# Two-layer Newton and spectral-convolution kernel: pacing the normalisation statistics of layer 0, and a round between dependent operations on different engines

## The chip, the cores and the metric

One Trainium2 chip, one of its cores. The metric is device time in microseconds of one execution, median over runs. TensorE is called PE, VectorE DVE, ScalarE ACT, GpSimd POOL and SyncE SP; PSUM is the matmul accumulator, eight banks.

## The reference

The input `x` has 32 batches of 32 channels of 128x128 float32 images. Each layer normalises and adds its result to its input:

```python
def _gn(v, G=16, eps=1e-5):
    ...
    return ((g - m) / jnp.sqrt(s + eps)).reshape(v.shape)

# layer 0: Newton iterations towards a matrix square root of each 128x128 image
normA = jnp.sqrt(jnp.sum(A2 * A2, axis=(1, 2)))
Y = A2 / normA[:, None, None]
...
for _ in range(NUM_ITER):
    T = 0.5 * (3.0 * I - jnp.matmul(Z, Y))
    Y = jnp.matmul(Y, T)
    Z = jnp.matmul(T, Z)
...
x = x + _L0_conv_ref(_gn(x))
# layer 1: FFT, 32x32 low modes mixed over channels, inverse FFT
x = x + _L1_conv_ref(_gn(x), L1_conv_weights1, L1_conv_weights2)
```

For this case only the shape of the work matters: layer 0 needs, before it can start on a batch, statistics of that batch's input (a sum of squares per channel and mean and variance per pair of channels, with two square roots on the way). Layer 1 needs the same kind of statistics of layer 0's output, with one square root, and then transforms, small channel products and an inverse transform.

## The kernel before, in words

**Sets.** A set is four channels of one batch: 8 sets a batch, 256 in all. `newton` (L398 on) takes a set through layer 0: ten groups of matmuls for a far set and twelve for a near one (below), almost all into one PSUM bank each, each read out by DVE (L280, L425) or ACT (L272, L404, L407, L418, L421) into the operand of the next. It yields between the groups.

**Rounds and lanes.** The main loop at the end of the function writes the program in rounds. In a round each of up to nine lanes advances its set by one step, and between the lanes other queues advance by a step: `norms` (a set's normalisation, `staged`), `preps` (statistics of layer 0, after lane 1), `specs` (statistics and spectrum of layer 1, after lane 2), `posts`, `prods` and `backs` (channel products and inverse transforms of layer 1). A `yield` in one of these generators ends its step, so what follows is written down a round later. A scheduler orders the instructions of each engine by the order of writing and by when it believes operands to be there; instructions in `kept(...)` keep their order. So each engine's queue is fixed before the run.

**Two stages.** The sets of batches 1 to 18 are "far": one transposition goes through DRAM and POOL (L373 to L386), nine lanes are in use and a set starts every 3 rounds (`FAR`). Those of batch 0 and of batches 19 to 31 are "near": that transposition is on PE, about five lanes are in use and a set starts every 5 rounds (`NEAR`). While `early` is open, up to the 158th finished set (`MORE`), extra buffers exist; then `change()` closes it and opens the buffers of layer 1's products and inverse transforms. That is the second stage here: from about 1,680 us on, layer 0's near sets run side by side with `wide_products`, `small_products` and `inverse` of layer 1. The batches of layer 1 go in groups of 20, 7, 3 and 2 (`GROUPS`); a group's products begin when the spectrum of its last batch is done.

**Statistics of layer 0.** `prep` (L185) does two batches at a time. It loads 16 pieces of 256 KB on ACT's DMA queue (L198, tile `xs`, four buffers, three loads ahead), takes two `bn_stats` of each (L206, one step a piece), then `moments` (two small matmuls, L170 and L214, and a few DVE operations), `root` (L154: a square root on ACT, four DVE operations), a reciprocal, `root` again, and the factors. Counted in the code, the results are there after 24 steps. `stage` (in the main part) adds a `prep` to the queue when the set named in `coming` is staged: for batches b, b+1 that is set 4 of batch b-2. They are needed when set 0 of batch b is staged, 12 sets later.

**Layer 1's part.** `settle` folds a finished set and takes its `bn_stats` (L443). `summed` (L484 on) and `spectrum` (L516 on) run in `specs` once a batch. In `summed` the DVE reciprocal L506 follows the ACT square root L505; in `spectrum` the small DVE operation L551 follows the ACT read-out L545 of the same tile. `inverse` reads four banks: the ACT copies L895 (tile `d`) take one half of each bank and the DVE additions L900 (tile `yt`) the other.

Of the kernel before, what the change touches and what calls it, by code (L numbers as in the profile page):

```python
# [37 lines left out]
B = 32  # L38
# [13 lines left out]
FIRST = GROUPS[0] - 1  # L52
# [16 lines left out]
def conv_preact_kernel(  # L69
# [56 lines left out]
    early = first.enter_context(tc.tile_pool(name="early", bufs=1, side="right"))  # L126
# [21 lines left out]
    def bank():  # L148
        return ps8.tile([P, 4, P], F32, tag="ps", name="ps")

    def root(v, n, tag):

        s0 = small.tile([P, n], F32, tag="root_0", name=f"{tag}_s0")
        nc.scalar.activation(s0, v, AF.Sqrt)  # L154
        q = small.tile([P, n], F32, tag="root_1", name=f"{tag}_q")
        nc.vector.reciprocal(q, s0)
        nc.vector.tensor_mul(q, q, v)
        nc.vector.tensor_tensor(q, q, s0, ALU.add)
        s = small.tile([P, n], F32, tag=f"{tag}_s", name=f"{tag}_s", bufs=2)
        nc.vector.tensor_scalar_mul(s, q, 0.5)  # L160
        return s
# [23 lines left out]
    def prep(bs, made):  # L185

        n = len(bs)
        nc_, ng = n * C, n * G
        first_b = bs[0]
        st = small.tile([P, ng, 6], F32, tag="a_st", name=f"a_st{first_b}", bufs=2)  # L190
        tiles = []
        parts = [(b, i) for b in bs for i in range(C // 4)]

        def load(k):
            b, i = parts[k]
            t = stp.tile([P, 2, 2 * P], F32, tag="xs", name=f"xs{b}_{i}")
            src = xs_in[b, :, 2 * i : 2 * i + 2].rearrange("p g h c -> p g (h c)")
            kept(nc.scalar.dma_start(out=t, in_=src))  # L198
            tiles.append(t)

        for k in range(3):
            load(k)
        yield
        for k in range(len(parts)):
            for j in range(2):
                nc.vector.bn_stats(st[:, 2 * k + j, :], tiles[k][:, j, :])  # L206
            yield
            if k + 3 < len(parts):
                load(k + 3)
        ms = small.tile([P, ng], F32, tag="a_ms", name=f"a_ms{first_b}")  # L210
        nm, d = yield from moments(st, ms, "a")
        yield from pause
        pq = bank()[:, 0, 0:nc_]
        nc.tensor.matmul(pq, avg_mean, d.rearrange("p g c -> p (g c)"), start=True, stop=True)  # L214

        v = small.tile([P, nc_ + ng], F32, tag="a_v", name=f"a_v{first_b}")
        nc.vector.tensor_scalar_mul(v[:, 0:nc_], pq, -512 / (P * P))
        yield
        vg = small.tile([P, ng], F32, tag="a_vg", name=f"a_vg{first_b}")
        nc.vector.tensor_reduce(  # L220
            vg, v[:, 0:nc_].rearrange("p (g c) -> p g c", c=2), AX.X, ALU.add
        )
        nc.vector.tensor_scalar(v[:, nc_:], vg, 0.5, EPS, ALU.mult, ALU.add)
        s = root(v, nc_ + ng, "a_r")
        iv = small.tile([P, nc_ + ng], F32, tag="a_inv", name=f"a_inv{first_b}")
        nc.vector.reciprocal(iv, s)
        yield

        sc = small.tile([P, nc_], F32, tag="a_sc", name=f"a_sc{first_b}", bufs=2)
        nc.vector.tensor_scalar_mul(sc, iv[:, 0:nc_], MS / P)  # L230
        nn = small.tile([P, ng, 2], F32, tag="a_d", name=f"a_n{first_b}")
        nc.vector.tensor_tensor(  # L232
            nn,
            s[:, 0:nc_].rearrange("p (g c) -> p g c", c=2),
            iv[:, nc_:, None].to_broadcast([P, ng, 2]),
            ALU.mult,
        )
        nn = nn.rearrange("p g c -> p (g c)")
        nc.vector.tensor_scalar_mul(nn, nn, P * (1.5 / (EYE * QF)) ** 2)
        sn = root(nn, nc_, "a_t")  # L240

        off = small.tile([P, ng, 2], F32, tag="a_off", name=f"a_off{first_b}", bufs=2)
        nc.vector.tensor_tensor(
            off,
            sc.rearrange("p (g c) -> p g c", c=2),
            nm[:, :, None].to_broadcast([P, ng, 2]),
            ALU.mult,
        )
        off = off.rearrange("p g c -> p (g c)")
        for k, b in enumerate(bs):  # L250
            g, c = slice(k * G, k * G + G), slice(k * C, k * C + C)
            made[b] = (nm[:, g], sc[:, c], off[:, c], sn[:, c])
        yield
# [60 lines left out]
    def is_far(b):  # L314
        return 0 < b < FIRST
# [168 lines left out]
    def summed(b, st):  # L484

        mq = small.tile([P, 2, G], F32, tag="b_mq", name=f"b_mq{b}")
        _, d = yield from moments(st, mq[:, 0, :], "b")
        yield

        nc.vector.tensor_reduce(mq[:, 1, :], d, AX.X, ALU.add)  # L490
        wide = small.tile([P, 2, G, 2], F32, tag="b_wide", name=f"b_wide{b}")
        nc.vector.tensor_copy(wide, mq[:, :, :, None].to_broadcast([P, 2, G, 2]))
        wide = wide.rearrange("p k g c -> p k (g c)")
        yield from pause
        pv = bank()[:, 0, :]
        for i in range(4):
            rows = slice(C * i, C * i + C)
            nc.tensor.matmul(pv[rows, 0:1], wide[:, 1, :], avg_v, start=True, stop=True)
        nc.tensor.matmul(pv[0:C, 1:2], wide[:, 0, :], avg_0, start=True, stop=True)
        v = small.tile([P, 2], F32, tag="b_v", name=f"b_v{b}")  # L500
        nc.vector.tensor_scalar(v[:, 0:1], pv[:, 0:1], 1.0, EPS, ALU.mult, ALU.add)
        nc.vector.tensor_copy(v[0:C, 1:2], pv[0:C, 1:2])
        yield
        s = small.tile([P, 3], F32, tag="b_r", name=f"b_r{b}")
        nc.scalar.activation(s[:, 0:1], v[:, 0:1], AF.Sqrt)  # L505
        nc.vector.reciprocal(s[:, 1:2], s[:, 0:1])  # L506
        nc.vector.tensor_scalar(
            s[:, 2:3], v[:, 0:1], s[:, 1:2], s[:, 1:2], ALU.mult, ALU.mult
        )
        nc.vector.tensor_scalar(s[:, 2:3], s[:, 2:3], -0.5, 1.5, ALU.mult, ALU.add)  # L510
        r = small.tile([P, 1], F32, tag="b_inv", name=f"b_inv{b}")
        nc.vector.tensor_mul(r, s[:, 1:2], s[:, 2:3])
        scales[b] = v, r
        yield

    def spectrum(b, u):  # L516
# [16 lines left out]
        for i in range(2):  # L533
# [7 lines left out]
        v, r = scales.pop(b)  # L541
# [6 lines left out]
            AF.Identity,  # L548
            scale=r,
        )  # L550
        nc.vector.scalar_tensor_tensor(  # L551
            spec[0:C, 0, 0, 0:1], v[0:C, 1:2], r[0:C], spec[0:C, 0, 0, 0:1], ALU.mult, ALU.add
        )
        yield
        i, j = where[b]
# [375 lines left out]
    rounds = 0  # L931
# [59 lines left out]
    def finish(queue):  # L991
        while queue:
            yield

    preps.append(prep([0], made))
    coming = [((0, 0), [1])] + [((b - 2, 4), [b, b + 1]) for b in range(2, B, 2)]
    fetch(*fetches.pop(0))
    stage()
    fetch(*fetches.pop(0))
    while todo or any(lanes) or posts or specs or prods or backs:  # L1000
        tail = not todo and not any(lanes)
        if early and len(settled) >= MORE:
            change()
        for i in range(LANES):
            step(norms)
            step(loads)
            far = todo and is_far(todo[0][0])
            under_way = [is_far(lane[0]) for lane in lanes if lane]
            room = far or under_way.count(False) + 0.6 * under_way.count(True) < LESS
            if lanes[i] is None and todo and room and rounds >= due:  # L1010
                due = max(due, rounds - 1) + (FAR if far else NEAR)
                while norms:
                    step(norms)
                b, g = todo.pop(0)
                xt = ready[0][0]
                lanes[i] = (b, g, xt, newton(g, made[b][3], *ready.pop(0), far, has_more(b, g)))
                if stages:
                    stage()
                if not todo:
                    loads.append(weights())  # L1020
            if lanes[i] is not None:
                b, g, xt, steps = lanes[i]
                if (b, g) == (B - 1, C // 4 - 1):
                    steps_of_last.append(rounds)
                if next(steps, lanes) is lanes:
                    lanes[i] = None
                    end(b, g, xt)
            if i == 1:
                step(preps)
            if i == 2 or tail:  # L1030
                step(specs)
            if i == 3 or tail:
                step(posts)
            if i == 0 and rounds % 3 or tail:
                step(prods)
            if i == 0 and (rounds % 3 == 0 or holding) or tail and not (posts or specs):
                step(backs)
        rounds += 1
# [69 lines left out]
```

## Time and profile before

| quantity | value |
|---|---|
| time, median of 3 runs | 3051.56 us (3039.80 to 3056.13) |
| the profiled execution's own time | 3040.36 us |
| its span, first to last instruction | 3038.6 us |
| PE busy | 2893.8 us (95%) |
| DVE busy | 2219.3 us (73%) |
| POOL busy | 1997.6 us (66%) |
| ACT busy | 1636.0 us (54%) |
| mean granted PE clock | 0.984 |
| DMA, mean rate | 209 GB/s |

The busy time of PE counts the time in which at least one matmul is under way, with modelled ends, so that the count of matmul instructions started in a stretch says more than the busy share. One float32 product of 128x128 by 128x128 is two such instructions. Times within the span are counted from its start.

### The profile page before, as it was taken

How to read it: one execution, taken by the hardware profiler on the slowest of the kernel's cores; microseconds unless marked ns; L12 is line 12 of the kernel's file. 1: busy time of each engine (PE TensorE's matmuls, PEld its weight loads, DVE VectorE, ACT ScalarE, POOL GpSimd, SP SyncE). 2: the span in 40 equal slices, each digit the busy share in tenths (PEclk: the TensorE clock that was granted, in tenths of full speed). 3: DMA queues.
4: the chain of work that ended last, by engine and by line, in shares of the span. 5: the costliest groups of instructions: out<-in, count | busy, mean ns of one | idle time of the engine just before them, and what ended most of it. 6: DMA issues, size and time to landing. Idle time of an engine off the chain costs nothing.

```text
span 3038.6 us, 73447 instructions
## 1 busy us (share of the span) xinstructions
PE 2893.8 (95%) x27076; PEld 2684.5 (88%) x27076; DVE 2219.3 (73%) x4255; ACT 1636.0 (54%) x4187; POOL 1997.6 (66%) x2312
## 2 busy tenths in 40 slices
PE   6999999999999999999999999899999998999994
PEld 6899999999999999999999889798898887899983
DVE  6778787978787878778776745876877765876664
ACT  3565656565655656566544445455454454555552
POOL 4567677667777676777766435667677774677453
PEclk9999999999999999999999999999999999999996
DMA  5476766667675767576742566667667767775676
GB/s 179 148 224 199 220 213 205 212 207 224 197 237 188 251 184 246 185 229 198 228 136 81 183 204 214 232 206 239 229 225 242 245 231 242 227 222 189 198 240 217
DMA packets 476659, 636.40 MB, mean 209 GB/s; under 512 B 97040, under 2 KB 257296, under 8 KB 476304
## 3 DMA queue, kind: packets, MB, share of 16 engines
q1 hardware_dynamic: 363408, 425.88, 43.3%
q10 hardware_dynamic: 112896, 205.83, 21.4%
q8 instruction: 217, 3.56, 0.5%
q14 instruction: 138, 1.13, 0.1%
HBM read 402.42 MB, written 229.11 MB: 208 GB/s over the span
## 4 chain that ended last, share of the span: by engine, by line
PE 75%; DMA 10%; DVE 9%; POOL 2%; issue 2%; ACT 2%; SPq 1%; ACTq 0%; DVEq 0%; POOLq 0%
PE ps L305 49%; PE ps L415 12%; PE ps L311 6%; DMA w<-turn 3%; DMA xs<-in_xs 3%; PE ps L461 2%; PE ps L883 2%; DMA or<-od 1%; PE ps L612 1%; DVE yt L900 1%; PE ps L865 1%; DVE a_st L206 1%; DVE v L280 1%; DVE turn L371 1%; PE ps L682 1%
## 5 line engine op out<-in xcount | busy, mean ns | idle before, releaser
L386 POOL TENSOR_TENSOR w<-w,r 128x512 f32<-128x512 f32 x288 | 366.2, 1275 | 316.2 <-DMA w<-turn 262.1
L305 PE MATMUL ps<-w,v 128*128 128x128 f32 x4096 | 554.4, 279 | 19.0 <-POOL w L386 12.1
L339 ACT ACTIVATE b<-b,a_off,a_sc 128x128 f32<-128x128 f32 x1024 | 467.3, 491 | 177.5 <-issue 45.6
L305 PEld LDWEIGHTS ps<-w,v 128*128 128x128 f32 x4096 | 504.6, 193 | 35.1 <-POOL w L386 16.2
L415 PE MATMUL ps<-my,q 128*128 128x256 f32 x2048 | 493.3, 384 | 7.8 <-DVE q L280 5.2
L280 DVE SCALAR_TENSOR_TENSOR q<-ps,eye 128x512 f32<-128x512 f32 x512 | 348.8, 681 | 187.4 <-PE ps L305 181.1
L438 POOL TENSOR_TENSOR fold<-xt 128x256 f32<-128x256 f32 x512 | 364.3, 732 | 162.8 <-DVE xt L425 133.2
L833 POOL TENSOR_TENSOR yt<-yt,d 128x512 f32<-128x512 f32 x248 | 309.9, 1277 | 174.3 <-ACT d L895 137.7
L415 PEld LDWEIGHTS ps<-my,q 128*128 128x128 f32 x2048 | 373.2, 192 | 53.3 <-DVE q L280 4.7
L346 POOL TENSOR_SCALAR x<-xt,a_nm,a_sc 128x128 f32<-128x128 f32 x736 | 322.3, 450 | 18.3 <-DVE a_n L232 18.3
L299 POOL TENSOR_TENSOR r<-mb,eye 128x512 f32<-128x512 f32 x112 | 142.6, 1274 | 288.6 <-ACT mb L272 278.8
L418 ACT ACTIVATE t<-ps 128x256 f32<-128x256 f32 x512 | 192.6, 384 | 237.3 <-PE ps L415 229.4
L421 ACT ACTIVATE y<-ps,a_t_s 128x128 f32<-128x128 f32 x1024 | 312.4, 372 | 0.0
L305 PE MATMUL ps<-my,q 128*128 128x128 f32 x2048 | 276.7, 278 | 6.0 <-ACT d L895 3.9
L305 PE MATMUL ps<-x,b 128*128 128x128 f32 x2048 | 275.6, 278 | 6.7 <-POOL x L346 5.7
L305 PE MATMUL ps<-my,mb 128*128 128x128 f32 x2048 | 275.9, 278 | 6.5 <-ACT d L895 5.2
L305 PE MATMUL ps<-x,q 128*128 128x128 f32 x2048 | 276.0, 278 | 1.8 <-DVE q L280 1.6
L206 DVE BATCH_NORM_STATS2 a_st<-xs 128x6 f32<-128x256 f32 x512 | 195.4, 412 | 112.6 <-DMA xs<-in_xs 112.0
L305 PE MATMUL ps<-q,t 128*128 128x128 f32 x2048 | 274.5, 277 | 3.2 <-ACT d L895 1.6
L305 PEld LDWEIGHTS ps<-my,q 128*128 128x128 f32 x2048 | 260.8, 193 | 17.4 <-ACT d L895 4.5
L404 ACT ACTIVATE my<-ps 128x512 f32<-128x512 f32 x256 | 152.7, 596 | 229.2 <-PE ps L305 211.1
L305 PE MATMUL ps<-y,t 128*128 128x128 f32 x2048 | 273.9, 277 | 1.9 <-DVE t L280 1.6
(138 smaller groups left out, 5540.3 us busy)
## 6 DMA issues: line engine op xcount, KB each, us to landing
turn<-turn SPq DMA_DIRECT2D x288, 256.0 KB
b<-in_x ACTq DMA_DIRECT2D x256, 256.0 KB
xt<-in_xt ACTq DMA_DIRECT2D x256, 256.0 KB
xs<-in_xs ACTq DMA_DIRECT2D x256, 256.0 KB
mid<-xt SPq DMA_DIRECT2D x256, 256.0 KB
yt<-mid SPq DMA_DIRECT2D x128, 512.0 KB
out<-yt SPq DMA_DIRECT2D x120, 512.0 KB
w<-turn SPq DMA_DIRECT2D x144, 256.0 KB
```

Of the source, the lines that this page charges most:

```text
L206: nc.vector.bn_stats(st[:, 2 * k + j, :], tiles[k][:, j, :])
L280: nc.vector.scalar_tensor_tensor(s, ps, f, t, ALU.mult, ALU.add)
L305: nc.tensor.matmul(ps[:, j, :], lhsT[:, j], rhs[:, j], start=True, stop=True)
L311: nc.tensor.transpose(ps[:, j, :], t[:, j, :], ident)
L339: nc.scalar.activation(t, x, AF.Identity, bias=offset[:, c], scale=scale[:, c])
L346: nc.gpsimd.tensor_scalar(m[:, j, :], xt[:, j, :], nm[:, c // 2 : c // 2 + 1], sc[:, c : c + 1], ALU.add, ALU.mult,)
L386: nc.gpsimd.tensor_tensor(w, w, r, ALU.add)
L415: nc.tensor.matmul(both[j // 2][:, j % 2], q[:, j], my[:, j], start=True, stop=True)
L418: nc.scalar.mul(w[:, 2 * h : 2 * h + 2, :], both[h][:, :, 1, :], 1 / (MS * QF))
L421: nc.scalar.mul(y[:, j, :], both[j // 2][:, j % 2, 0, :], sn[:, c : c + 1])
L438: nc.gpsimd.tensor_tensor(f[:, :, 64 * half : 64 * half + 64], xt[:, :, 0:64], xt[:, :, 64:128], op)
L833: engine.tensor_tensor(yh, yh, d, op)
```

## The change

Three things. (1) In the second stage, `preps` gets its step in every second round only (`early or rounds % 2`). (2) For the batches from `FIRST` = 19 on, the statistics are put in the queue at set 2 of batch b-2 where it was set 4, two sets sooner; `b` goes over even numbers, so this concerns batches 20, 22, ... 30. (3) In both stages a `yield` stands between an operation on one engine and the next on another: in `prep` ahead of each of the two square roots (DVE to ACT) and behind each (ACT to DVE), in `summed` behind its square root, in `spectrum` between L545 and L551. `root` becomes a generator for it.

```diff
         nc.scalar.activation(s0, v, AF.Sqrt)
+        yield
         q = small.tile([P, n], F32, tag="root_1", name=f"{tag}_q")
         nc.vector.reciprocal(q, s0)
...
-        s = root(v, nc_ + ng, "a_r")
+        yield
+        s = yield from root(v, nc_ + ng, "a_r")
...
-        sn = root(nn, nc_, "a_t")
+        yield
+        sn = yield from root(nn, nc_, "a_t")
...
         nc.scalar.activation(s[:, 0:1], v[:, 0:1], AF.Sqrt)
+        yield
         nc.vector.reciprocal(s[:, 1:2], s[:, 0:1])
...
             AF.Identity,
             scale=r,
         )
+        yield
         nc.vector.scalar_tensor_tensor(
...
-    coming = [((0, 0), [1])] + [((b - 2, 4), [b, b + 1]) for b in range(2, B, 2)]
+    coming = [((0, 0), [1])] + [((b - 2, 4 if b < FIRST else 2), [b, b + 1]) for b in range(2, B, 2)]
...
-            if i == 1:
+            if i == 1 and (early or rounds % 2):
                 step(preps)
```

No instruction is added or removed: DVE has 4,257 shown instructions in the program before and after, and only their order differs.

## The prediction, made before the changed kernel was run

> **What bounds the kernel now.** I read the page's totals first, then the waits of PE by stage, then a table of windows around the statistics of layer 0, then the instructions in order of time inside one of them.
>
> ```profile
> PE 2893.8 (95%) x27076; PEld 2684.5 (88%) x27076; DVE 2219.3 (73%) x4255; ACT 1636.0 (54%) x4187; POOL 1997.6 (66%) x2312
> ```
>
> PE sets the time. Its idle time (145 us) is all that a change of order can win. From 150 to 1400 us there is next to none: PE is busy for 603.3 of 610 and 635.2 of 640 us, and its longest class of waits there is 4.6 us in nine pieces. So nothing is to be won in the first stage. In the second, the eight windows below alternate between the 68 to 78 us in which `prep` runs (from its first L206 to its second square root) and the time between. Columns: length, then busy us and instructions of PE, weight load, DVE, ACT, POOL, then granted clock, DMA share, GB/s.
>
> ```profile
> 1901.00:1979.00 78.00, 67.47 (x545) 59.44 (x545) 65.62 (x134) 33.63 (x90) 48.17 (x57) 0.91 0.65 220
> 1979.00:2115.00 136.00, 135.52 (x1215) 124.86 (x1218) 96.46 (x163) 71.98 (x191) 104.53 (x124) 1.00 0.68 230
> 2115.00:2193.00 78.00, 69.74 (x581) 61.20 (x578) 61.87 (x134) 33.37 (x90) 48.67 (x57) 0.93 0.69 235
> 2193.00:2334.00 141.00, 140.88 (x1256) 129.97 (x1256) 97.09 (x166) 75.90 (x200) 108.83 (x127) 1.00 0.67 228
> 2334.00:2402.00 68.00, 61.62 (x533) 53.15 (x532) 58.09 (x134) 32.92 (x89) 46.95 (x56) 1.00 0.77 253
> 2402.00:2470.00 68.00, 67.67 (x618) 61.91 (x617) 48.59 (x92) 34.48 (x94) 54.44 (x63) 1.00 0.60 202
> 2563.00:2639.00 76.00, 65.28 (x556) 57.94 (x555) 59.04 (x131) 39.56 (x93) 41.52 (x49) 0.96 0.75 235
> 2639.00:2800.00 161.00, 158.95 (x1414) 145.35 (x1413) 114.06 (x201) 92.09 (x229) 126.01 (x150) 1.00 0.64 213
> ```
>
> Without `prep`, 4503 matmuls start in 506 us: 8.90 per us. With it, 2215 in 300 us: 7.38. At the calm rate they would take 2215 / 8.90 = 248.9 us, so the four bursts cost **51 us**: 35.9 us of PE idle (300 less 67.47, 69.74, 61.62, 65.28), the rest matmuls at a lower clock and small gaps. How `prep` does it is seen at the start of the third burst, in order of time:
>
> ```profile
> 2335.23 0.43 DVE L206 BATCH_NORM_STATS2 a_st<-xs 128x6 f32<-128x256 f32 x1 [4.47 <-DMA xs<-in_xs]
> 2335.57 1.27 DVE L900 TENSOR_TENSOR yt<-ps,yt 128x512 f32<-128x512 f32 x2
> 2336.28 0.97 ACT L895 COPY d<-ps 128x256 f32<-128x256 f32 x3 [4.77 <-DVE yt L900]
> ...
> 2336.71 1.13 PE L415 MATMUL ps<-my,q 128*128 128x256 f32 x4 [2.43 <-ACT d L895]
> ```
>
> The columns are start, us, engine, line, operation, and in brackets the idle time before with what ended it. DVE stood 4.47 us at the head of its queue for a late piece of `xs`; behind it stood the addition L900, behind that the ACT copy of the same bank, behind that a matmul that needed the bank. In the four bursts DVE waited for `xs` 10.3, 10.2, 11.8 and 2.9 us: 35.2 us.
>
> **What the Trainium skill says.** "PSUM — Partial Sum Buffer", section "Engine vs sequencer instructions": the queues of ScalarE, VectorE and GpSimd are strictly first in, first out. The trace agrees: 4.47 us above, with L900 stuck behind L206. The same page, "PSUM bank collisions raise a hardware error": two engines are kept off one bank, two readers too. It agrees: the ACT copy waits 4.77 us for the DVE addition on the same bank. "TensorE: Matmul & The Clock Gate", Part 1: an idle PE drops to half clock until it has been busy for a window. The trace agrees in kind: 0.91, 0.93 and 0.96 in three bursts, 1.00 in every calm window. "DMA: Bandwidth & Descriptors", "Issuing engines are not separate DMA queues": loads issued by ACT share the 16 engines with SP's transfers. That fits `xs` being late at DMA shares of 0.65 to 0.77.
>
> **The change part by part.**
>
> (1) Half pace. Of the 51 us I take off the 6.6 us for which PE waits at L865 for a DMA of layer 1's products in the fourth burst: 44 us hang on `prep`. A burst's own DVE work is its DVE time less what the matmuls usually bring with them, 0.079 us each (96.46/1215): 65.62 - 43.1, and so on, about 17 us. Sixteen sets lie between two bursts' starts (1901 to 2115: 214 us), so a set is about 12.6 us without the loss, and a round, five to a set, 2.5 us. `prep` now has 28 steps to its results (24, and four new yields), so 56 rounds, some 125 us as the first and last few are short; 17/125 = 0.14 on top of a calm DVE share of 0.71 gives 0.85. That share is harmless where it occurs: in 1389 to 1419 us DVE is busy for 25.56 of 30 us and PE for 29.85, and in 2019 to 2049 us 24.66 and 29.52. The loads: 16 pieces of 256 KB in about 45 us are 93 GB/s on top of 228 to 230; they become about 50, and a load has six rounds (15 us) from issue to use where it had three. I keep a quarter of the loss for pieces that are still late, an estimate between none and all: 11 us. What limits next is PE's own stream, which in the calm windows is idle for at most 1.3%. Gain **33 us**; ends 0 and 51 (the whole rate difference).
>
> The order of instructions in the changed program bears this out: up to now 10 or 11 L206 stand between the ends of two sets, over three sets; now 4 to 8 over six sets (finished sets 174 to 179, 190 to 195, and so on).
>
> (2) Two sets sooner. Without it 56 rounds would have to fit in 12 sets, 60 rounds; now 14 sets, 70 rounds. In the new order the last root stands at finished set 183, 198, 215 and 230, and the first set of the new batch is staged some six finished sets before 192, 208, 224, 240: at least two sets, 25 us, to spare. **0 us**; if that cover went, normalisation would hold PE up by up to one round a pair. Each step carries its DMA issue on ACT's queue (0.334 us, 16 a pair), moved past `staged`'s activations and `fetch`'s loads there; none goes through SP or POOL. The pair 20, 21 falls in the first stage at full pace, and batches 22, 23 cost PE little now (1680 to 1745 us: 3.0 us idle, all for a weight DMA of L612). 0 both.
>
> (3) The yields. They take no instruction away. The waits they aim at are ACT's for L154 (27.2 and 19.7 us in all) and DVE's for L551 (28.1 us, 10.3 of it in 2700 to 2950 us). No PE wait of over 2 us leads back to either in the list, ACT is 54% busy, and PE is full in the first stage. **0**, at best -6, the second-stage share of L551's. Their cost: a spectrum is ready two rounds later (`summed` one, `spectrum` one), 5 us, and with it a group's products and, in the order, some inverse transforms (one stands at set 250 that stood at 249). PE has other work meanwhile, except after the last sets, where it is idle for 42 of 90 us anyway. **+1**, ends 0 and +6.
>
> Sum: -33 + 0 + 0 + 1 = **-32 us**. Against its own time of 3040.4 us the profiled execution would take 3008. It is 11.2 us under the median of the runs, 3051.6; what I predict is that median less 32: **3019 us**. Small stalls move whenever the order does; three runs of one program already spread over 16 us.
>
> **Rivals.**
>
> *The waits stay.* If `xs` is late because 512 KB stores stand in front of it on the DMA engines, and not because pieces follow each other closely, each of the 16 loads may still be late. For it: DMA shares of 0.65 to 0.77. Against it: calm windows run at 0.60 to 0.68 without harm, and the loads have twice the time. If three quarters stay: 3051.6 - 11 + 1 = 3042 us.
>
> *Twice as long at the same rate.* Slower. If a stretch with `prep` in it loses at today's rate whatever its density, because each step that waits empties the few near lanes and they need the rest of the round to fill, the loss doubles with the length: 44 us more, 3096 us. It decides from 44/600 = 0.073 us lost per us of `prep` (now 44/300 = 0.147). For it: near sets have five lanes, and in the first stage, with nine, DVE waits 54 us for `xs` and PE feels nothing. Against it: the order puts other DVE work between the pieces, and 0.85 DVE share is met elsewhere without loss.
>
> *The end moves.* If late spectra push the last three inverse transforms behind the last sets, 5 us, it only trims the gain: 3024 us. This I count in the forecast.
>
> **How the numbers follow.** Forecast 0.69, with its own range 2998 to 3036; waits stay 0.22 (3036 to 3058); twice as long 0.09. Up to 0.5% (15 us, about what a measurement can tell from no change) either way is 3036 to 3067. So faster 0.69, same 0.22, slower 0.09. Cutting 0.05 below and the slow case with a little of the second above leaves 2996 to 3054.
>
> **What would show it.** Right: windows of 125 us with L206 in them at 8.5 matmuls per us or more; DVE's waits for `xs` after 1900 us well under 35 us; PE idle there down by some 25 us, with the clock at 0.98 or more; the first stage unchanged. The yields: fewer L551 and L154 waits without any PE time for it. Wrong: the same `xs` waits at the new places, PE waiting for L346 or L339 of a batch whose factors are late, or a longer stretch after 2950 us.

## The result, and the profile after

| | before | changed |
|---|---|---|
| median of 12 runs each | 3045.17 us | 3050.37 us |
| ratio of the runs, 95% interval | | 1.0015 (0.9999 to 1.0031) |
| the profiled execution: time, span | 3040.36, 3038.6 us | 3058.61, 3056.7 us |

No change that can be told from none, where 32 us less was forecast. With twelve runs the median of before is 6 us lower than with the three shown ahead of the prediction. The changed kernel's profiled execution is 8 us above its own median, that of before 5 us below; so between these two traces some 13 of the 18 us are the choice of execution, and what follows goes by places, counts and waits more than by the two ends. Every wait, count and lead below is read from one profiled execution of its kernel.

The first page line of the changed kernel:

```profile
PE 2901.3 (95%) x27076; PEld 2697.1 (88%) x27076; DVE 2238.3 (73%) x4255; ACT 1638.1 (54%) x4187; POOL 1999.1 (65%) x2312
```

The same work (4255 DVE instructions on this page, as on that of before), and PE as busy as it was. Windows of the changed kernel, with `prep` (first, third, fifth) and between, columns as in the prediction:

```profile
1866.00:1996.00 130.00, 119.45 (x1005) 108.38 (x1005) 95.56 (x186) 60.71 (x162) 89.05 (x104) 0.95 0.65 215
1996.00:2082.00 86.00, 85.88 (x780) 78.57 (x779) 66.10 (x118) 47.63 (x128) 67.47 (x78) 1.00 0.73 243
2082.00:2208.00 126.00, 116.60 (x990) 105.70 (x989) 91.37 (x177) 60.15 (x159) 82.62 (x98) 0.95 0.68 226
2208.00:2301.00 93.00, 89.57 (x787) 81.95 (x786) 69.83 (x119) 47.17 (x125) 68.17 (x82) 0.98 0.65 219
2301.00:2427.00 126.00, 115.78 (x994) 104.83 (x993) 93.89 (x182) 60.21 (x159) 90.69 (x106) 0.97 0.70 230
```

The statistics did spread as announced: three stretches of 126 to 130 us in place of 78, 78 and 68. (The fourth lies on top of small products of layer 1 and is left out here, before and after.) But PE is still idle in them: 30.2 us in 382, where it was 25.2 in 224. The three stretches start 2989 matmuls; at the calm rate of before, 8.90 per us, that is 335.8 us, so they lose **46 us**. Before they lost 224 - 1659/8.90 = **38 us**. (The two calm stretches between them start 1567 matmuls in 179 us, so they lose 3 us by the same count.) The loss per us fell from 0.168 to 0.121, and there are more us. The clock is down in them as it was (0.95, 0.95, 0.97).

What ends DVE's waits from 1640 us to the end, the line of the list for `xs`, first before, then changed (waits in us, how many, the longest):

```profile
DVE a_st L206 <- DMA xs<-in_xs: 39.9, 20, 6.3
```

```profile
DVE a_st L207 <- DMA xs<-in_xs: 74.4, 34, 5.7
```

At half the pace DVE waits nearly **twice as long** for the pieces. Why is seen in the changed kernel in order of time, filtered to the loads (on ACT's queue, L199) and DVE's use of them (L207), and the three operations behind the last:

```profile
2306.31 0.44 ACTq L199 DMA_DIRECT2D xs<-in_xs  x1
...
2309.74 0.33 ACTq L199 DMA_DIRECT2D xs<-in_xs  x1
2311.55 0.75 DVE L207 BATCH_NORM_STATS2 a_st<-xs 128x6 f32<-128x256 f32 x2 [2.11 <-DMA xs<-in_xs]
...
2316.39 0.43 DVE L207 BATCH_NORM_STATS2 a_st<-xs 128x6 f32<-128x256 f32 x1 [2.30 <-DMA xs<-in_xs]
2316.61 0.36 ACTq L199 DMA_DIRECT2D xs<-in_xs  x1
...
2321.33 0.43 ACTq L199 DMA_DIRECT2D xs<-in_xs  x1
2321.98 0.43 DVE L207 BATCH_NORM_STATS2 a_st<-xs 128x6 f32<-128x256 f32 x1 [1.80 <-DMA xs<-in_xs]
...
2329.41 0.43 DVE L207 BATCH_NORM_STATS2 a_st<-xs 128x6 f32<-128x256 f32 x1 [4.90 <-DMA xs<-in_xs]
2329.75 1.87 DVE L905 TENSOR_TENSOR yt<-ps,yt 128x512 f32<-128x512 f32 x3
2330.46 0.97 ACT L900 COPY d<-ps 128x256 f32<-128x256 f32 x3 [5.89 <-DVE yt L905]
2330.88 1.46 PE L418 MATMUL ps<-my,q 128*128 128x256 f32 x4 [3.55 <-ACT d L900]
```

The loads are 3.4 to 6.9 us apart, so the pace is the slow one. But the piece issued at 2306.31 is used at 2311.55, that of 2316.61 at 2321.98, that of 2321.33 at 2329.41: between these loads and their uses at most one other load is issued. The chain behind the last is the known one, L905, then L900, then a matmul that waits 3.55 us.

How far apart the program writes them is seen in `prep`:

```python
        for k in range(len(parts)):
            for j in range(2):
                nc.vector.bn_stats(st[:, 2 * k + j, :], tiles[k][:, j, :])
            yield
            if k + 3 < len(parts):
                load(k + 3)
```

Behind each `yield` a new step begins, so `load(k + 3)` belongs to the step that takes the statistics of piece k + 1. Its use comes two steps later, and two other loads are written in between. The prediction counts three steps, and so do two of the expectations below; it is two. With the prediction's round of 2.5 us that is two rounds or 5 us at full pace, four rounds or 10 us at half pace.

Taken over the 80 pieces of batches 22 to 31 in each trace (start of the load's issue to start of its first use, in order), the mean lead is **5.46 us before and 4.99 us changed**. Before, that is about what is written; in the changed kernel it is half of it. For 70 of the 80 pieces two other loads should stand between load and use (the last two of each 16 have fewer behind them). In the trace of before there are at least two for 34 of the 70, in the changed kernel for 7, and for 42 there is none. The pace did not lengthen the lead. Two pieces of before, in the same filter (issued at 2336.89 and 2337.96, used at 2342.63 and 2343.39):

```profile
2336.89 0.33 ACTq L198 DMA_DIRECT2D xs<-in_xs  x1
...
2337.96 0.33 ACTq L198 DMA_DIRECT2D xs<-in_xs  x1
...
2342.63 0.75 DVE L206 BATCH_NORM_STATS2 a_st<-xs 128x6 f32<-128x256 f32 x2
...
2343.39 0.42 DVE L206 BATCH_NORM_STATS2 a_st<-xs 128x6 f32<-128x256 f32 x1
```

So the theory, A: DVE's order is not the order of writing. The scheduler moves a statistics operation up to the place where it believes the load has landed, and the chip lands it later; a slower pace does not lengthen that lead, it only isolates each piece, so that more of them are waited for. What the scheduler believes stands in no trace; that part is inferred from the order. Rivals: B, loads are late whatever their lead, because of other transfers, or the yields take back what the pace wins; C, DVE's work costs PE and not its waiting, or loss goes with the length of the stretch.

### The profile page after: what moved, and what is told of

The parts are those of the page before. It is cut to its first block, busy times and chain, and to the rows that moved or that the text cites. A ratio compares the mean times of both kernels' runs of the same rounds, so it can differ in the third digit from the quotient of the medians.

```text
span 3056.7 us, 73392 instructions
## 1 busy us (share of the span) xinstructions
PE 2901.3 (95%) x27076; PEld 2697.1 (88%) x27076; DVE 2238.3 (73%) x4255; ACT 1638.1 (54%) x4187; POOL 1999.1 (65%) x2312
## 4 chain that ended last, share of the span: by engine, by line
PE 76%; DMA 11%; DVE 5%; POOL 3%; ACT 2%; issue 2%; SPq 1%; ACTq 0%; DVEq 0%; POOLq 0%
PE ps L308 50%; PE ps L418 12%; PE ps L314 6%; DMA xs<-in_xs 4%; PE ps L464 2%; DMA w<-turn 1%; PE ps L888 1%; DMA or<-od 1%; PE ps L617 1%; POOL yt L838 1%; PE ps L870 1%; PE ps L529 1%; DVE yt L905 1%; DMA plain<-in_wk 1%; DVE a_st L207 1%
## 5 line engine op out<-in xcount | busy, mean ns | idle before, releaser
L207 DVE BATCH_NORM_STATS2 a_st<-xs 128x6 f32<-128x256 f32 x512 | 195.8, 412 | 139.1 <-DMA xs<-in_xs 138.6
```

## The experiments

Ratios are to the kernel before, run beside it on the same chip, with the 95% interval; medians of different rows can come from different chips, so rows are compared by ratio, and times in us are worked out from it; leads as above; waits of DVE for `xs` from 1640 us on, from the list of waits.

| kernel | median us | ratio (95%) | lead us | waits us |
|---|---|---|---|---|
| before | 3045.2 | 1 | 5.46 | 39.9 |
| changed | 3050.4 | 1.0015 (0.9999 to 1.0031) | 4.99 | 74.4 |
| pace only | 3056.8 | 1.0041 (1.0024 to 1.0057) | 5.11 | 70.7 |
| yields only | 3041.6 | 0.9977 (0.9963 to 0.9992) | 5.43 | 34.3 |
| changed, operations kept | 3020.1 | 0.9909 (0.9890 to 0.9928) | 10.94 | 1.1 |
| same, constant input | 3013.9 | 0.9888 (0.9869 to 0.9907) | 10.96 | none |
| before, operations kept | 3030.9 | 0.9954 (0.9937 to 0.9972) | 7.19 | 11.0 |
| pace only, kept | 3020.2 | 0.9922 (0.9900 to 0.9944) | 11.11 | 2.8 |
| yields only, kept | 3022.2 | 0.9924 (0.9903 to 0.9945) | 7.22 | 12.1 |
| changed, kept in both stages | 3013.6 | 0.9894 (0.9873 to 0.9914) | 11.04 | 3.9 |
| changed, slower still | 3039.1 | 0.9956 (0.9941 to 0.9971) | 5.03 | 65.7 |
| changed, two pieces ahead | 3059.0 | 1.0030 (1.0009 to 1.0050) | 4.92 | 84.4 |

**The parts apart.** Before, with the edits of parts (1) and (2) alone, half pace and two sets sooner; here and below they go together and are called the pace:

```diff
-    coming = [((0, 0), [1])] + [((b - 2, 4), [b, b + 1]) for b in range(2, B, 2)]
+    coming = [((0, 0), [1])] + [((b - 2, 4 if b < FIRST else 2), [b, b + 1]) for b in range(2, B, 2)]
...
-            if i == 1:
+            if i == 1 and (early or rounds % 2):
```

> Parts 1 and 2 alone: half pace and two sets sooner, no yields added. Theory A (the order on DVE is made by a scheduler that pulls each statistics operation up to where it believes its load landed, so the lead of a load, issue to use about 5 us in before and after, is not lengthened by a slower pace): DVE's waits for xs after 1,650 us stay near those of the change (about 75 us), no gain; time within 8 us of before. Theory B (the pace does pay, and the yields take it back later): 15 to 30 us faster than before. Theory C (twice as long at the same rate): 15 us or more slower than before.

Measured: +0.41%, about 12 us **slower**, waits 70.7 us. The pace by itself is a loss. B falls in its form that the yields take a gain back: there is none. The waits are near the 75 us that A named, but the time is outside the 8 us that A allowed. It is short of the 15 us of C, but the interval reaches 17 us, so this run alone does not rule C out.

The changed kernel with these two edits undone, the yields alone:

> Part 3 alone. The trace of the change is 12 us ahead of before at the end of set 151, where only the yields can act, and falls back by 14 us after the last statistics (sets 228 to 255). Theory A: the yields win up to 12 us in the first stage; in the second they lose little, so 5 to 12 us faster than before. Theory B: the yields delay layer 1's spectra and lose in the second stage, so as slow as the change or slower. Theory C: both are chance of single executions; within 5 us of before.

Measured: 0.23% or 7 us faster, waits 34.3 us, near the 39.9 of before. That is what A said, but the interval, 2 to 11 us, reaches into C's 5 us. Where: in 150 to 1400 us, where only the yields can act, PE starts 10,335 matmuls before, 10,336 with pace only, 10,415 with the yields:

```profile
150.00:1400.00 1250.00, 1243.63 (x10415) 1179.19 (x10415) 1003.08 (x1924) 755.13 (x1957) 906.78 (x999) 1.00 0.70 215
```

This is the line of yields only; 80 of 10,335 in 1250 us are 10 us. But the gain is not steady: over all traces here the four without yields have 10,318 to 10,336, the eight with them 10,337 to 10,420, the latter in the mean 49 more, or 6 us.

**The lead made longer.** The changed kernel with each statistics operation of the second stage bound to its written place in DVE's order, behind all that was written before it on DVE:

```diff
-                nc.vector.bn_stats(st[:, 2 * k + j, :], tiles[k][:, j, :])
+                ins = nc.vector.bn_stats(st[:, 2 * k + j, :], tiles[k][:, j, :])
+                if not early:
+                    kept(ins)
```

> The changed kernel with each statistics operation of the second stage kept behind what was written before it on DVE, so that it is queued a full three steps (six rounds, some 15 us) after its load. Theory A: waits for xs after 1,650 us fall from about 75 us to under 20, PE idle in those windows falls, 20 to 35 us faster than before. Theory B (loads are late because of other transfers, whatever the lead): waits stay above 50 us and the time within 8 us of the change. Theory C (it is DVE's work, not its waiting, that costs PE): waits fall and the time stays within 8 us of the change.

Measured: 0.91% faster than before, about 28 us, and by ratio some 32 us under the change. The lead is 10.94 us, near the four written rounds (the 15 us in the expectation came from the miscount). At least two other loads stand between for 56 of the 70 pieces, and at least one for all. The piece issued at 2287.23, for example, is used at 2299.78:

```profile
2287.23 0.44 ACTq L199 DMA_DIRECT2D xs<-in_xs  x1
...
2291.31 0.34 ACTq L199 DMA_DIRECT2D xs<-in_xs  x1
...
2298.47 0.34 ACTq L199 DMA_DIRECT2D xs<-in_xs  x1
...
2299.78 0.74 DVE L207 BATCH_NORM_STATS2 a_st<-xs 128x6 f32<-128x256 f32 x2
```

The waits are all but gone:

```profile
DVE a_st L207 <- DMA xs<-in_xs: 1.1, 2, 0.9
```

Its windows, with `prep` and between:

```profile
1870.00:1990.00 120.00, 117.66 (x1045) 107.16 (x1044) 99.07 (x194) 62.95 (x169) 90.90 (x106) 1.00 0.73 242
1990.00:2072.00 82.00, 81.66 (x742) 74.79 (x743) 62.27 (x109) 45.60 (x120) 63.39 (x73) 1.00 0.73 243
2072.00:2193.00 121.00, 115.79 (x1023) 105.58 (x1022) 97.25 (x185) 60.48 (x159) 88.59 (x106) 0.99 0.74 249
...
2283.00:2398.00 115.00, 112.69 (x1013) 103.11 (x1011) 96.04 (x186) 60.42 (x159) 91.66 (x107) 1.00 0.75 253
```

With `prep`, 3081 matmuls in 356 us are 8.65 per us, and the loss is 356 - 3081/8.90 = 10 us where it was 46. PE is idle for 9.9 us, the clock is back at 0.99 to 1.00, and DVE is busier in these stretches (0.80 to 0.84) than in the changed kernel's (0.73 to 0.75). So a DVE share of 0.84 does no harm, and C falls. The DMA share is no lower either (0.73 to 0.75), and next to nothing is late: B falls too. A holds in what it says of lead, waits and time. One thing this run does not part: the binding can also move other DVE work against the statistics. Constant data in the free order, which would take the waits away without the binding, was not run.

The same with a constant tile in place of the loaded pieces, which are still loaded. This kernel leaves out layer 0's statistics of batches 22 to 31, so it does not compute the reference:

```diff
+                src = tiles[k][:, j, :] if early else tab[:, 0:256]
+                ins = nc.vector.bn_stats(st[:, 2 * k + j, :], src)
```

> As the kernel with kept statistics, but in the second stage these operations read a constant tile of the same width in place of the loaded pieces, which are still loaded: layer 0's statistics of batches 22 to 31 are left out. No wait for xs is possible. Theory A: at most 8 us faster than the kernel with kept statistics on real data. Theory B: 20 us or more faster than that. Theory C: within 8 us of the change.

Measured: 3013.9 against 3020.1 us, with overlapping intervals, within the 8 us that A allowed. What waiting for `xs` still costs with the operations kept is 6 us or nothing.

**Is the pace then needed?** The same binding in the kernel before, in pace only and in yields only.

> The kernel before with the statistics operations of the second stage kept in their place on DVE: full pace, no yields added. Theory A1 (the waits are the whole cost of the bursts): the lead from issue to use grows from 5.4 to 7 or 8 us, the waits after 1,650 us fall from 40 to under 10, and the time falls by 20 to 30 us without any change of pace. Theory A2 (half of the cost is DVE's own density in the burst): waits fall as far, the time by 8 to 18 us, and pace is worth 10 us more once the waits are gone.

> Half pace and two sets sooner, statistics operations kept in their place, no yields added. Beside the kernel with all three (3020 us) it shows the yields' share, beside full pace with kept operations the pace's share. Theory A1: equal to full pace with kept operations within 6 us. Theory A2: 8 us or more faster than that. The yields' share, from the run with yields alone, is 4 to 5 us, so 3024 us in A2.

> Full pace with the yields, statistics operations kept in their place. Theory A1: 3015 to 3022 us. Theory A2: 3025 to 3035 us, about 5 us under full pace without yields.

Measured: full pace with the binding gains 0.46%, 14 us; its lead is 7.19 us, where 5 are written and 5.46 were measured in the free order, and 11.0 us of waits remain, just over the 10 expected. With half pace it is 0.78%, 24 us, with a lead of 11.11 and 2.8 us of waits. The numbers are those of A2 in size for the first two (though what remains at full pace is partly waits, not density alone, so the two are not fully parted). For the yields at full pace A2 gave 3025 to 3035 us, and 3022.2 was measured, at the edge of A1. Set out by ratio, in per cent of the time before:

| | full pace | half pace |
|---|---|---|
| free order, no yields | 0 | +0.41 |
| free order, yields | -0.23 | +0.15 |
| kept, no yields | -0.46 | -0.78 |
| kept, yields | -0.76 | -0.91 |

The half pace **costs** 0.4% while the order is free, with or without yields, and **pays** 0.3% or about 10 us once the operations keep their place (3030.9 and 3020.2 us, with intervals that just overlap; with the yields it is 0.15%, which is within the intervals).

**Both stages kept.**

> The changed kernel with the statistics operations kept in their place in both stages. PE is busy over 99% of the first stage although DVE waits there about 54 us for xs, so both theories expect these waits to fall to under 25 us and the time to stay within 5 us of 3020 us.

Measured: waits in 150 to 1640 us fall from the 54.0 us of the changed kernel to 21.6, as expected; the time, 3013.6 us, is just outside the 5 us around 3020 that were expected. By ratio it is 0.15% or 5 us under the version kept in one stage, with intervals that overlap. The first stage gives at most little, as PE is full there. With 1.06% (0.86 to 1.27) this is the best version seen that computes the reference.

**Two controls of the theory.** If the written pace or distance set the lead, slowing further or loading less far ahead would move it. As written the first has two steps in five rounds, about 12.5 us, and the second one step, two rounds or 5 us, half of the change's 10.

```diff
-            if i == 1 and (early or rounds % 2):
+            if i == 1 and (early or rounds % 5 in (0, 2)):
```

with the statistics begun at set 0 of batch b-2, and, in another kernel,

```diff
-        for k in range(3):
+        for k in range(2):
             load(k)
...
-            if k + 3 < len(parts):
-                load(k + 3)
+            if k + 2 < len(parts):
+                load(k + 2)
```

> The changed kernel, operations not kept, with the statistics spread further: a step in two rounds of five, begun four sets sooner than before. If pace were the lever, waits for xs after 1,650 us would fall below the 74 us of the change and the time with them. Theory A (each operation is queued right behind its load whatever the pace): the lead stays at 4 to 6 us, the waits between 65 and 95 us, the time within 8 us of the change.

> The changed kernel, operations not kept, with loads two pieces ahead instead of three. If the written distance set the lead, a third of it would go, with more waiting and some 5 to 15 us more time. Theory A: the lead is set by the scheduler's belief about landing, not by the written distance, so it stays at 4 to 6 us, waits within 15 us of the change's 74, time within 6 us of the change.

Measured: leads of 5.03 and 4.92 us, waits of 65.7 and 84.4 us. Written at 5, 10 or 12.5 us, the lead stays at 5 us; only binding lengthened it. In the second, time and waits fit A (by ratio 5 us over the change). In the first the waits fit (65.7, at the edge), but the time does not: 0.44% faster than before, some 18 us faster than the change by ratio, where A allowed 8. Waits under the change's 74 us and less time with them are also what was expected if pace were the lever; the lead of 5.03 us alone speaks against that. So the time is not a function of these waits alone. That kernel starts batches 22 and 23 at sets 155 to 159, before layer 1's products begin, and its trace gains 13 us against that of the change between the ends of sets 192 and 228 (in order of ending, counted from 0); what it does better there was not isolated.

Loads four or five pieces ahead in a free order were not run; what they would do is left open.

## Why the prediction was wrong, by its own steps

**Where PE loses: right.** Bursts of `prep` lose 51 us by the same count, through L206, L900, L895 and the bank. With the waits taken away the loss of three stretches fell from 46 to 10 us.

**Step (1), half pace: the step that failed.** The prediction said "a load has six rounds (15 us) from issue to use where it had three". This is wrong in two ways. It miscounted: as written it is four rounds (10 us) where it was two (5 us). And it took the distance as written for the distance on the engine: the measured lead is 5.46 us before and 4.99 us with the change, so it did not double; it did not grow at all. The mean lead of before, near the written 5 us, gives no warning of the second error; it only fits the count of three badly. The order in the same trace did give one: for only 34 of 70 pieces did two other loads stand between load and use. The order that the prediction had read tells how many L206 lie between the ends of two sets, and nothing of where their loads stand. So three quarters of the loss did not go: in the four stretches with `prep` DVE's waits for `xs` rose from 35.2 us to 69.4 (20.4, 12.0, 21.3 and 15.7).

With the operations kept in the written order, two steps behind their loads, the gain is 28 us (forecast 32), the rate 8.65 (forecast "8.5 or more"), and DVE's share 0.80 to 0.84 (forecast 0.85). That the sum comes so near is partly luck, as it is made of other terms. The lead is 10.94 us and not 15. The binding gives 14 us at full pace already, half pace some 10 more, where step (1) put 33, and the yields some 4.

**Why it even costs.** At full pace one late piece delays those behind it, which are then ready: 20 waits for 80 pieces. At half pace each is placed just behind its own load: 34 waits. The mean lead hardly differs. That part is read from the traces, not tried by itself. The cost does not follow the waits in proportion either: in three stretches of each trace they rose from 32.3 to 53.7 us, and PE's idle time from 25.2 to 30.2 us.

**Step (2), two sets sooner: 0, not contradicted.** It was never run without half pace. In the trace of the change no wait on the factors of a batch is among PE's longest in the second stage.

**Step (3), yields: wrong in sign and place, small.** Forecast +1 us; measured -7 us alone (-2 to -11). By the counts of matmuls most of the gain, some 6 us, is in the first stage, which the prediction had called full. DVE's waits at the operation after the spectrum's read-out (L551 before, L556 changed) fell after 1640 us from 20.0 to 8.8 us as meant. Which of the yields frees PE in the first stage stays open.

**Rivals.** "The waits stay" named the right outcome (3042 us, with no change to be measured) for the wrong reason: it laid them on transfers in front, and with a longer lead there is next to no wait left at a higher DMA share. What makes a single load take 5 to 8 us was not parted. "Twice as long at the same rate" decides from 0.073 us lost per us; measured 0.121 over three stretches, so this rival had the sign: the loss grew, by 8 us, though not by the 44 us that it put. But the rate is not fixed by the lanes: with the same lanes and the operations kept it is 10 us in 356, 0.03.

**Left open.** From the end of set 228 to that of set 255, counted as above, the profiled executions with half pace or less lose 5 to 15 us against before, with full pace 2 to 5; the end of the last `prep` falls there, and the rest is unexplained.

## What to carry to other kernels

Prefetch distance in a scheduled program is the distance between issue and use on the engines' queues, not in the source. First count the written distance step by step: three pieces ahead were two steps here. Then measure issue to use of the loads in the trace before pricing a change of pace, and count how many other loads stand between each load and its use: where there are fewer than written, the order is not the written one, and a mean lead that looks right does not show it. A late load whose use stands at the head of DVE's queue holds up what stands behind it, as at 2329.41, and here neither a slower pace nor another written distance moved the lead, until the operations were bound to their place. The same edit can change its sign with that: half pace cost 0.4% before the binding and gained up to 0.3% after it.

## What the runs showed of the hardware that was not expected

In the stretch shown, 256 KB loads that were waited for took 5.2 to 8.1 us from issue to use (2306.31 to 2311.55, 2321.33 to 2329.41) at a mean DMA share of 0.70. And where PE stalled for 30.2 us in 382, the longest stalls being 2 to 4 us, the granted clock was 0.95 to 0.97, against 0.99 to 1.00 where 9.9 us of idle time were left: by the count of matmuls a third of the 46 us lost there is not idle time of PE at all.
